# A graph-network layer on one core: bias times std0 as a TensorE product, relu on ScalarE, weights on GpSimd, and another order of issue

## The chip, the cores and the metric

The kernel runs on one core of a Trainium2 chip. The metric is the device time of one execution, in microseconds (us). An iteration below is one turn of the kernel's main loop; a block is ten iterations.

## The reference, cut to what matters

There are 128 graphs of 64 nodes with 128 features, and a 0/1 adjacency matrix for each. An edge (i, j) carries a message, a three-layer network on the two nodes' features; messages of a node's edges are summed, and a second network of the same form updates the node.

```python
def _mlp(x, w0, b0, g0, be0, w1, b1, g1, be1, w2, b2):
    h = _layernorm(jax.nn.relu(x @ w0 + b0), g0, be0)
    h = _layernorm(jax.nn.relu(h @ w1 + b1), g1, be1)
    return h @ w2 + b2
messages = _mlp(concat(f_i, f_j), *msg) * coupling_matrix[..., None]
agg = jnp.sum(messages, axis=2)
updated = x + _mlp(concat(x, agg), *upd)
```

## The kernel before, in words

Only real edges are computed. Two graphs make a pair `p` (64 pairs) with up to 640 edges for each of its graphs; a chunk `n` (160 of them) is 512 edges; five chunks hold two pairs and share one layer-norm step `q`; a block `b` (16) is eight graphs, that is ten chunks. One iteration of the main loop (L721 to L751) issues one chunk's work of every stage, each stage at its own distance: `marks` (which node an edge belongs to, a product on TensorE into the bank `mk`), `compare` (VectorE, makes the 0/1 matrix `s`), `layer0` (two float32r products of 512 columns into `hps`, relu on ScalarE into `h`), `stats0` (four transposes into `hT`, four `bn_stats` on VectorE), `layer1` (four float32 products into `z`, then on VectorE one custom operation that adds `sdb` and takes the relu into `y`, then four `bn_stats`). Here std0 does not divide h: layer 1 is computed on the unnormalized h, and its bias is multiplied by std0 instead. `shift1` makes that product `sdb` on GpSimd, chunk by chunk.

After a step's five chunks, `node_marks` (TensorE) and `weights` (ten ScalarE operations a pair, scaled by 1/std1) give the weights with which `reduce` (20 TensorE instructions a pair) sums y over a node's edges. Per block come the preparation (`load_adj`, `load_x`, `rank`, `count`, `place`, `steps`, `turn`, `rows`) and the update network (`sums_out` to `finish`). `make_tp` (GpSimd) makes a pair's row pointers `tp`.

The order is written out by hand. Each engine executes its instructions in the order of issue. Work beside the chunk stages is put into a plan, `at(n, place, ...)`, and run at iteration `n` in the places `a` (first in the iteration), `m`, `r`, `x`, `x1`, `x2` and `e` (last). `L1`, the distance of layer 1 behind the first chunk stage, is 8. Each of `mk`, `hps`, `hT`, `z`, `ys` and `mu` has one PSUM bank, `ma` has two. Before the loop a prologue prepares block 0; thirteen steps that derive weights (`derive_weights`) run one after another at iterations 1 to 5, and after the loop the overflow flag is computed.

Of the kernel before, what the change touches and what calls it, by code (L numbers as in the profile page):

```python
# [18 lines left out]
EPS = 1e-5  # L19
# [4 lines left out]
def tile_gnn(  # L24
# [82 lines left out]
    nc.vector.memset(eps2_c, EPS * EPS)  # L107
    mean_m = const.tile([P, P], F32, name="mean_m")
    nc.vector.memset(mean_m, 1.0 / C)

# [24 lines left out]
    nc.gpsimd.iota(cmpt[N:P, :], pattern=[[0, 4], [1, CAP]], base=1, channel_multiplier=0,  # L135
                   allow_small_or_imprecise_dtypes=True)
    nc.vector.memset(cmpt[0:N, :], 1.0)
    first = const.tile([P, PB, N], F32, name="first")
    nc.vector.memset(first, 1.0)
    nc.vector.memset(first[:, :, 0:1], 0.0)  # L140

    w0a = mat(mw0[0:C, :], "w0a")
    w0b = mat(mw0[C:2 * C, :], "w0b")
    b0r = row(mb0, "b0r")
    b0c = col(mb0, "b0c")
    w1 = mat(mw1, "w1")
    g0c = col(mg0, "g0c")
    be0c = col(mbe0, "be0c")
    b1r = row(mb1, "b1r")
    w2 = mat(mw2, "w2")  # L150
    g1c = col(mg1, "g1c")
    be1c = col(mbe1, "be1c")
    b2r = row(mb2, "b2r")
    u0a = mat(uw0[0:C, :], "u0a")
    u0b = mat(uw0[C:2 * C, :], "u0b")
    u1 = mat(uw1, "u1")
    u2 = mat(uw2, "u2")
    ub = [row(v, f"ub{i}r") for i, v in enumerate((ub0, ub1, ub2))]
    ug = [col(v, f"ug{i}c") for i, v in enumerate((ug0, ug1))]
    ube = [col(v, f"ube{i}c") for i, v in enumerate((ube0, ube1))]  # L160
# [5 lines left out]
    def derive_weights(bank):  # L166


        def centred(w, g, name):

            wg = const.tile([P, C], F32, name=name + "_g")
            nc.vector.tensor_scalar(wg, w, g, None, op0=ALU.mult)
            ps = bank()
            nc.tensor.matmul(ps[:, :C], lhsT=mean_m, rhs=wg, start=True, stop=True)
            wc = const.tile([P, C], F32, name=name)
            nc.vector.tensor_tensor(wc, wg, ps[:, :C], op=ALU.subtract)
            return wc

        def shift(w, be, bias, name):

            beb = const.tile([P, P], F32, name=name + "_b")
            nc.vector.tensor_copy(beb, be.to_broadcast([P, P]))
            ps = bank()
            nc.tensor.matmul(ps[:, :C], lhsT=beb, rhs=w, start=True, stop=False)
            nc.tensor.matmul(ps[:, :C], lhsT=ones_row, rhs=bias, start=False, stop=True)
            t = const.tile([P, C], F32, name=name)
            nc.vector.tensor_copy(t, ps[:, :C])
            return t

        def spread(bias, name):  # L190
            ps = bank()
            nc.tensor.matmul(ps[:, :C], lhsT=ones_row, rhs=bias, start=True, stop=True)
            t = const.tile([P, C], F32, name=name)
            nc.vector.tensor_copy(t, ps[:, :C])
            return t

        def turned(w, name):
            ps = bank()
            nc.tensor.transpose(ps[:, :C], w, ident)
            t = const.tile([P, C], F32, name=name)  # L200
            nc.vector.tensor_copy(t, ps[:, :C])
            return t

        def times(wT, name):
            ps = bank()
            nc.tensor.matmul(ps[:, :C], lhsT=wT, rhs=u0b, start=True, stop=True)
            t = const.tile([P, C], F32, name=name)
            nc.vector.tensor_copy(t, ps[:, :C])
            return t

        W["w1c"] = centred(w1, g0c, "w1c")
        yield
        W["b1b"] = shift(w1, be0c, b1r, "b1b")
        yield

        w2c = centred(w2, g1c, "w2c")
        yield
        w2cT = turned(w2c, "w2cT")
        yield
        W["w2u"] = times(w2cT, "w2u")  # L220
        yield
        c2b = shift(w2, be1c, b2r, "c2b")
        yield
# [12 lines left out]
        W["cu2b"] = shift(u2, ube[1], ub[2], "cu2b")
# [55 lines left out]
    def edge_path(es):  # L292
# [3 lines left out]
        tpp = es.enter_context(tc.tile_pool(name="tpp", bufs=9))  # L296
        sp = es.enter_context(tc.tile_pool(name="sp", bufs=3))
        hp = es.enter_context(tc.tile_pool(name="hp", bufs=10))
        yp = es.enter_context(tc.tile_pool(name="yp", bufs=12))
        sbp = es.enter_context(tc.tile_pool(name="sbp", bufs=3))  # L300
        wp = es.enter_context(tc.tile_pool(name="wp", bufs=3))
        updp = es.enter_context(tc.tile_pool(name="upd", bufs=1))
        stp = es.enter_context(tc.tile_pool(name="stp", bufs=4))
# [27 lines left out]
        TP, S, H, ST0, V0, SD, SDB, Y, ST1, Q, WT, YS, MK = ({} for _ in range(13))  # L331


        def load_adj(b):
            an = blkp.tile([P, PB, N], F32, name="an", bufs=2)
            nc.sync.dma_start(an, adjp[:, b * PB:(b + 1) * PB, :])
            blocks[b]["an"] = an

        def load_x(b):
            xn = blkp.tile([P, PB, C], F32, name="xn", bufs=5)  # L340
# [155 lines left out]

        def root_of(q):
            SD[q] = root0(stp, V0[q], QT, "m20")

        def shift1(n):  # L500

            q, c = divmod(n, QC)
            SDB[n] = sbp.tile([P, CH, C], F32, name="sdb")
            nc.gpsimd.tensor_tensor(  # L504
                SDB[n], bc(W["b1b"], CH),
                SD[q][:, CH * c:CH * c + CH].unsqueeze(2).to_broadcast([P, CH, C]), op=ALU.mult)

        def layer1(n):
            q, c = divmod(n, QC)
            ps = ps_z.tile([P, CH, C], F32, name="z")  # L510
            h = H.pop(n)
            for t in range(CH):
                nc.tensor.matmul(ps[:, t, :], lhsT=h[:, t * P:(t + 1) * P], rhs=W["w1c"],  # L513
                                 start=True, stop=True)
            Y[n] = yp.tile([P, CH, C], F32, name="y")
            add_relu(Y[n], ps, SDB.pop(n))
            if c == 0:
                ST1[q] = stp.tile([P, QT, 6], F32, name="st1", bufs=2)
            for t in range(CH):
                nc.vector.bn_stats(ST1[q][:, CH * c + t, :], Y[n][:, t, :])  # L520

# [7 lines left out]
        def node_marks(p):  # L529

            WT[p] = []
            for t in range(TG):
                if t % 4 == 0:
                    ps = abank()
                WT[p].append(ps[:, t % 4 * P:(t % 4 + 1) * P])
                nc.tensor.matmul(WT[p][t], lhsT=TP[p][:, t * P:(t + 1) * P],  # L536
                                 rhs=pick.rearrange("p g m -> p (g m)"), start=True, stop=True)
            del TP[p]

        def weights(p):  # L540
# [98 lines left out]
        L1 = QC + 3  # L639
        for b in range(NB):  # L640
            o = b * CPB
            if b > 1:
                at(o - 17, "a", load_adj, b)
                at(o - 13, "a", load_x, b)
            if b > 0:
                at(o - 9, "m", rank, b)
                at(o - 9, "x", count, b)
                at(o - 8, "a", count_out, b)
                at(o - 8, "e", place, b)
# [282 lines left out]
```

## Time and profile before

| | us |
|---|---|
| three runs, median (lowest, highest) | 832.88 (831.65, 836.93) |
| the profiled execution, its own time | 837.1 |
| its span, first to last instruction | 835.4 |
| TensorE busy in the span | 658.4 (79%) |
| VectorE busy | 585.8 (70%) |
| GpSimd busy | 546.6 (65%) |
| ScalarE busy | 341.0 (41%) |

The mean granted TensorE clock is 0.924 of full speed. Matmuls are pipelined and the trace models their ends, so the duration of one is mostly its latency; what a stage costs TensorE in a dense stretch is read from one start to the next. "Idle before" names what an engine waited for.

### The profile page before, as it was taken

Reading aid. Unit: us, or ns where it says so; the run is one execution under the profiler, and the core shown is the slowest. Engines: PE = TensorE matmul, PEld = TensorE weight load, DVE = VectorE, ACT = ScalarE, POOL = GpSimd, SP = SyncE. Lnnn points to the kernel's source line nnn. Section 1 sums busy time; section 2 is a strip of 40 time slices with the busy share of each in tenths; the row PEclk is TensorE's granted clock in tenths of the full one; section 3 lists DMA queues with packets and bytes.
Section 4 is the critical chain, followed back from the end, with each engine's and each line's share of the span. In section 5 each row is a group of like instructions: output and inputs, shape, how many; then the busy total and the mean of one; then the engine's idle time right before and its main releaser. Section 6 shows DMA issues by size and latency. Waiting matters only on the chain.

```text
span 835.4 us, 15966 instructions
## 1 busy us (share of the span) xinstructions
PE 658.4 (79%) x5667; PEld 572.7 (69%) x5667; DVE 585.8 (70%) x1975; ACT 341.0 (41%) x1074; POOL 546.6 (65%) x1003
## 2 busy tenths in 40 slices
PE   4796878887887888788788877878778778878864
PEld 2575767776776787677677766767667666768753
DVE  3468766868677787877678676867768787777722
ACT  2133442444344344434534444444434443443431
POOL 5347555677766676776766667776666777665532
PEclk9999988899899999989999989999999999998966
DMA  3000000010101001010100001010000000000000
GB/s 82 20 1 19 2 1 7 1 33 1 33 2 27 7 2 33 1 33 2 31 2 22 12 2 33 1 33 1 26 8 1 27 2 14 1 13 2 14 10 19
DMA packets 27887, 12.08 MB, mean 14 GB/s; under 512 B 10390, under 2 KB 27804, under 8 KB 27804
## 3 DMA queue, kind: packets, MB, share of 16 engines
q1 hardware_dynamic: 26496, 11.01, 4.9%
q8 instruction: 46, 0.75, 0.4%
q14 instruction: 37, 0.30, 0.1%
q10 hardware_dynamic: 1308, 0.01, 0.1%
HBM read 6.82 MB, written 4.19 MB: 13 GB/s over the span
## 4 chain that ended last, share of the span: by engine, by line
PE 48%; POOL 17%; DVE 16%; ACT 14%; issue 3%; DMA 1%; ACTq 0%; DVEq 0%; POOLq 0%
PE z L513 13%; ACT w L547 7%; PE hps L482 6%; PE hT L491 6%; PE ys L560 6%; PE mk L467 4%; PE mu L589 4%; ACT h L485 4%; PE ma L412 4%; DVE y L245 3%; DVE st L520 3%; DVE st L495 2%; POOL tp L451 2%; DVE s L474 2%; PE mu L426 2%
## 5 line engine op out<-in xcount | busy, mean ns | idle before, releaser
L485 ACT ACTIVATE h<-hps,b0c 128x512 f32<-128x512 f32 x160 | 109.7, 686 | 287.2 <-PE hps L482 287.1
L504 POOL TENSOR_TENSOR sdb<-b1b,m_sd 128x512 f32<-128x512 f32 x160 | 164.6, 1038 | 84.7 <-ACT m_sd L262 84.7
L513 PE MATMUL z<-w1c,h 128*128 128x128 f32 x1280 | 186.2, 292 | 9.6 <-DVE y L245 8.4
L513 PEld LDWEIGHTS z<-w1c,h 128*128 128x128 f32 x1280 | 170.3, 207 | 17.0 <-DVE y L245 16.4
L474 DVE TENSOR_TENSOR s<-mk,cmpt 128x512 fp32r<-128x512 f32 x160 | 109.2, 682 | 80.8 <-PE mk L467 80.5
L495 DVE BATCH_NORM_STATS2 st<-hT 128x6 f32<-128x128 f32 x640 | 141.4, 285 | 4.3 <-PE hT L491 4.3
L520 DVE BATCH_NORM_STATS2 st<-y 128x6 f32<-128x128 f32 x640 | 139.6, 281 | 5.5
L245 DVE CUSTOM_DVE_ANT_0 y<-z,sdb 128x512 f32<-128x512 f32 x160 | 107.4, 671 | 50.3 <-POOL sdb L504 36.1
L547 ACT ACTIVATE w<-ma,m_q 128x64 f32<-128x64 f32 x640 | 137.3, 344 | 2.2 <-PE ma L536 1.8
L451 POOL TENSOR_SCALAR tp<-slot,cumall 128x640 f16<-128x640 f16 x64 | 120.5, 1883 | 0.0
L491 PE MATMUL hT<-ident,h 128*128 128x128 f32 x640 | 111.5, 303 | 7.4 <-ACT h L485 7.4
L491 PEld LDWEIGHTS hT<-ident,h 128*128 128x128 f32 x640 | 86.2, 157 | 30.6 <-ACT h L485 13.9
L252 POOL TENSOR_TENSOR m_d<-st 128x20 f32<-128x20 f32 x64 | 15.9, 249 | 129.8 <-DVE st L520 74.7
L482 PE MATMUL hps<-s,abl 128*128 128x512 f32 (+3 forms) x256 | 96.2, 386 | 0.0
L560 PE MATMUL ys<-y,w 128*64 128x128 f32 x1280 | 87.1, 284 | 0.0
L482 PE MATMUL hps<-s,abh 128*128 128x512 f32 (+3 forms) x256 | 81.0, 335 | 0.0
L560 PEld LDWEIGHTS ys<-y,w 128*64 128x64 f32 x1280 | 71.3, 141 | 9.5 <-issue 4.6
L467 PE MATMUL mk<-tp,qs 128*128 128x512 f16 (+3 forms) x256 | 68.8, 333 | 6.1 <-POOL tp L451 6.1
L536 PE MATMUL ma<-pick,tp 128*128 128x128 f16 x320 | 32.2, 225 | 40.1 <-ACT uhT L418 40.1
L467 PEld LDWEIGHTS <-qs 128*128 128x128 f16 x256 | 21.7, 110 | 52.2 <-issue 49.6
L482 PEld LDWEIGHTS hps<-s,abl 128*128 128x128 f32 x256 | 52.5, 205 | 0.0
L482 PEld LDWEIGHTS hps<-s,abh 128*128 128x128 f32 x256 | 52.1, 204 | 0.0
(166 smaller groups left out, 960.4 us busy)
## 6 DMA issues: line engine op xcount, KB each, us to landing
xn<-in_x_dram SPq DMA_DIRECT2D x16, 256.0 KB, 3.2
out_dram<-uo SPq DMA_DIRECT2D x16, 256.0 KB, 2.4
an<-in_adj_dram SPq DMA_DIRECT2D x16, 128.0 KB, 2.2
w<-in_L_gnn_msg_w_dram SPq DMA_DIRECT2D x2, 64.0 KB, 2.3
u<-in_L_gnn_upd_w_dram SPq DMA_DIRECT2D x2, 64.0 KB, 2.2
w0a<-in_L_gnn_msg_w_dram SPq DMA_DIRECT2D x1, 64.0 KB, 1.8
w0b<-in_L_gnn_msg_w_dram SPq DMA_DIRECT2D x1, 64.0 KB, 2.3
u0a<-in_L_gnn_upd_w_dram SPq DMA_DIRECT2D x1, 64.0 KB, 2.2
```

The lines of the kernel that those rows point to most:

```text
L245: nc.vector._custom_dve(TENSOR_ADD_SAT, out=o, in0=ps, in1=sb, s0=BIG, s1=0.0)
L451: nc.gpsimd.tensor_scalar(tp, slot, cumall[:, p:p + 1], None, op0=ALU.is_lt)
L474: nc.vector.tensor_tensor(S[n], MK.pop(n), cmpt[:, o:o + CH * P], op=ALU.is_equal)
L482: nc.tensor.matmul(ps[:, c:c + w], lhsT=ab[:, g % 4, :], rhs=s[:, c:c + w], start=(k == 0), stop=(k == 1))
L485: nc.scalar.activation(H[n], ps, AF.Relu, bias=b0c)
L491: nc.tensor.transpose(ps[:, t, :], H[n][:, t * P:(t + 1) * P], ident)
L495: nc.vector.bn_stats(ST0[q][:, CH * c + t, :], ps[:, t, :])
L504: nc.gpsimd.tensor_tensor(SDB[n], bc(W["b1b"], CH), SD[q][:, CH * c:CH * c + CH].unsqueeze(2).to_broadcast([P, CH, C]), op=ALU.mult)
L513: nc.tensor.matmul(ps[:, t, :], lhsT=h[:, t * P:(t + 1) * P], rhs=W["w1c"], start=True, stop=True)
L520: nc.vector.bn_stats(ST1[q][:, CH * c + t, :], Y[n][:, t, :])
L547: nc.scalar.activation(w[:, t, g, :], WT[p][t][:, g * N:(g + 1) * N], AF.Copy, scale=Q[q][:, k:k + 1])
L560: nc.tensor.matmul(YS[b][g * N:(g + 1) * N, k, :], lhsT=w[:, t, g, :], rhs=y, start=(t == 0), stop=(t == TG - 1))
```

## The change

- Std0 of a step (80 rows: its 20 tiles, high and low parts, twice) is transposed by TensorE (`root_of`, `turn_root`, `root_out`), and a first product of `layer1` with a table `b1t` (made once, `bias_table`) puts bias times std0 into the bank `z`; the four products add to it. ScalarE takes the relu. `shift1` and the VectorE operation are gone.
- `weights`: ScalarE copies the node marks out (`node_marks_out`, 384 and 256 columns), GpSimd multiplies (two instructions a pair).
- `make_tp` moves from GpSimd to VectorE.
- `L1` is 10; in an iteration the order is `a`, `m`, layer 1, layer 0, stats0, marks and compare (two chunks ahead), stats1, then the rest. Planned steps that hand over to another engine have an iteration between them; the last step is at iteration 193 (183 before). `reduce` of both pairs of a step runs in one iteration.
- The derivation's steps run one an iteration, with their scaling on GpSimd; the flag's steps are planned before the last chunks.
- The first blocks' loads go first, and the small loads move from ScalarE's queue to SP's. Several pools have more buffers.

```diff
-    def col(ap, name, eng=nc.scalar):
+    def col(ap, name, eng=nc.sync):
...
+    load_first(0)
     w0a = mat(mw0[0:C, :], "w0a")
...
+    nc.scalar.activation(eps2_c, eps_c, AF.Sqrt)
+    nc.scalar.activation(eps2_c, eps_c, AF.Square)
...
-            nc.gpsimd.tensor_scalar(tp, slot, cumall[:, p:p + 1], None, op0=ALU.is_lt)
+            nc.vector.tensor_scalar(tp, slot, cumall[:, p:p + 1], None, op0=ALU.is_lt)
...
         def root_of(q):
-            SD[q] = root0(stp, V0[q], QT, "m20")
-
-        def shift1(n):
-
-            q, c = divmod(n, QC)
-            SDB[n] = sbp.tile([P, CH, C], F32, name="sdb")
-            nc.gpsimd.tensor_tensor(
-                SDB[n], bc(W["b1b"], CH),
-                SD[q][:, CH * c:CH * c + CH].unsqueeze(2).to_broadcast([P, CH, C]), op=ALU.mult)
+            sd = root0(stp, V0[q], QT, "m20")
+            SH[q] = lp.tile([P, 4, QT], F32R, name="sh", bufs=2)
+            sdb = sd.unsqueeze(1).to_broadcast([P, 2, QT])
+            nc.scalar.copy(SH[q][:, 0:2, :], sdb)
+            nc.gpsimd.tensor_tensor(SH[q][:, 2:4, :], sdb, SH[q][:, 0:2, :].bitcast(F32),
+                                    op=ALU.subtract)
+
+        def turn_root(q):
+            SD[q] = abank()
+            nc.tensor.transpose(SD[q][0:4 * QT, 0:P],
+                                SH.pop(q).rearrange("p j t -> p (j t)").bitcast(F32), ident)
+
+        def root_out(q):
+            t = lp.tile([4 * QT, P], F32R, name="sdT")
+            nc.scalar.copy(t, SD[q][0:4 * QT, 0:P])
+            SD[q] = t
...
+            nc.tensor.matmul(ps, lhsT=SD[q], rhs=W["b1t"][:, CH * c:CH * c + CH, :], start=True,
+                             stop=False, skip_group_check=True)
             for t in range(CH):
                 nc.tensor.matmul(ps[:, t, :], lhsT=h[:, t * P:(t + 1) * P], rhs=W["w1c"],
-                                 start=True, stop=True)
+                                 start=False, stop=True, skip_group_check=True)
             Y[n] = yp.tile([P, CH, C], F32, name="y")
-            add_relu(Y[n], ps, SDB.pop(n))
+            nc.scalar.activation(Y[n], ps, AF.Relu)
+
+        def stats1(n):
...
+        def node_marks_out(p):
+            o = wp.tile([P, TG, 2, N], F16, name="oh")
+            for ps, t, n in zip(OH[p], (0, 3), (3, TG - 3)):
+                nc.scalar.copy(o[:, t:t + n].rearrange("p t g m -> p (t g m)"), ps[:, 0:n * P])
+            OH[p] = o
+
         def weights(p):
...
-            for t in range(TG):
-                for g in range(2):
-                    k = (2 * h + g) * TG + t
-                    nc.scalar.activation(w[:, t, g, :], WT[p][t][:, g * N:(g + 1) * N], AF.Copy,
-                                         scale=Q[q][:, k:k + 1])
+            for g in range(2):
+                k = (2 * h + g) * TG
+                nc.gpsimd.tensor_tensor(
+                    w[:, :, g, :], OH[p][:, :, g, :],
+                    Q[q][:, k:k + TG].unsqueeze(2).to_broadcast([P, TG, N]), op=ALU.mult)
...
-        L1 = QC + 3
+        L1 = 2 * QC
...
+            w = p // 2 * QC + L1 + QC + p % 2
+            at(w + 1, "x", node_marks, p)
+            at(w + 2, "a", node_marks_out, p)
+            at(w + 3, "e1", weights, p)
+            at(p // 2 * QC + L1 + 2 * QC, "x1", reduce, p)
         for q in range(NQ):
...
+            n = q * QC + QC
+            at(n, "e1", var0_of, q)
+            at(n + 2, "a", root_of, q)
+            at(n + 3, "x", turn_root, q)
+            at(n + 4, "a", root_out, q)
+            at(n + L1, "e1", var1_step, q)
+            at(n + L1 + 2, "a", root1_of, q)
+            at(n + L1 + 2, "m", inverse_of, q)
...
         for n in range(last + 1):
             run(n, "a")
+            run(n, "m")
+            if 0 <= n - L1 < NCHK:
+                layer1(n - L1)
             if n < NCHK:
...
+                layer0(n)
+            if 0 <= n - 1 < NCHK:
+                stats0(n - 1)
+            if n + 2 < NCHK:
+                marks(n + 2)
+                compare(n + 2)
+            if 0 <= n - L1 < NCHK:
+                stats1(n - L1)
+            for k in ("x", "x1", "x2", "e1", "e"):
                 run(n, k)
```

## Rows read from the trace of the kernel before

**Rows 1.** Page: busy time (share) and instructions of each engine.

```profile
PE 658.4 (79%) x5667; PEld 572.7 (69%) x5667; DVE 585.8 (70%) x1975; ACT 341.0 (41%) x1074; POOL 546.6 (65%) x1003
```

**Rows 2.** Timeline of ScalarE: relu of chunks 0, 10, 60, 70, 159.

```profile
20.42 0.69 ACT L485 ACTIVATE h<-hps,b0c 128x512 f32<-128x512 f32 x1 [0.80 <-PE hps L482]
...
65.07 0.69 ACT L485 ACTIVATE h<-hps,b0c 128x512 f32<-128x512 f32 x1 [1.53 <-PE hps L482]
...
301.84 0.69 ACT L485 ACTIVATE h<-hps,b0c 128x512 f32<-128x512 f32 x1 [0.49 <-PE hps L482]
...
349.56 0.69 ACT L485 ACTIVATE h<-hps,b0c 128x512 f32<-128x512 f32 x1 [0.49 <-PE hps L482]
...
774.50 0.69 ACT L485 ACTIVATE h<-hps,b0c 128x512 f32<-128x512 f32 x1 [0.93 <-PE hps L482]
```

**Rows 3.** Stretches of 4 us: busy PE, PEld, DVE, ACT, POOL; clock, DMA.

```profile
316.00:320.00 4.00, 1.59 (x9) 1.36 (x7) 1.24 (x6) 2.92 (x12) 3.87 (x6) 0.83 0.34 90
320.00:324.00 4.00, 4.00 (x28) 3.02 (x28) 3.06 (x11) 1.66 (x4) 4.00 (x4) 0.75 0.00 0
...
332.00:336.00 4.00, 4.00 (x53) 3.54 (x52) 3.93 (x14) 0.69 (x1) 1.26 (x6) 1.00 0.00 0
```

**Rows 4.** Waits: who waited for whom, us in total, times, longest.

```profile
PEld ma L412 <- ACT w L547: 91.1, 44, 2.9
POOL sdb L504 <- ACT m_sd L262: 84.7, 32, 3.3
```

**Rows 5.** Timeline of TensorE in a dense stretch (start, duration).

```profile
341.27 0.42 PE L482 MATMUL hps<-s,abl 128*128 128x384 f32 x1
...
341.87 1.10 PE L589 MATMUL mu<-u1c,uhT 128*128 128x128 f32 x8
342.81 0.38 PE L467 MATMUL mk<-tp,qs 128*128 128x512 f16 x1
343.03 0.60 PE L491 MATMUL hT<-ident,h 128*128 128x128 f32 x4
343.46 1.06 PE L513 MATMUL z<-w1c,h 128*128 128x128 f32 x8
344.27 0.48 PE L482 MATMUL hps<-s,abl 128*128 128x512 f32 x1
344.59 0.40 PE L482 MATMUL hps<-s,abh 128*128 128x512 f32 x1
344.83 0.46 PE L536 MATMUL ma<-pick,tp 128*128 128x128 f16 x5
345.21 1.31 PE L560 MATMUL ys<-y,w 128*64 128x128 f32 x20
346.36 0.27 PE L426 MATMUL mu<-w0a,xnT 128*64 128x128 f32 x1
...
347.33 0.39 PE L467 MATMUL mk<-tp,qs 128*128 128x128 f16 x2
```

**Rows 6.** Page: groups of instructions: busy us, mean ns of one, idle before.

```profile
L485 ACT ACTIVATE h<-hps,b0c 128x512 f32<-128x512 f32 x160 | 109.7, 686 | 287.2 <-PE hps L482 287.1
L504 POOL TENSOR_TENSOR sdb<-b1b,m_sd 128x512 f32<-128x512 f32 x160 | 164.6, 1038 | 84.7 <-ACT m_sd L262 84.7
...
L474 DVE TENSOR_TENSOR s<-mk,cmpt 128x512 fp32r<-128x512 f32 x160 | 109.2, 682 | 80.8 <-PE mk L467 80.5
L495 DVE BATCH_NORM_STATS2 st<-hT 128x6 f32<-128x128 f32 x640 | 141.4, 285 | 4.3 <-PE hT L491 4.3
...
L245 DVE CUSTOM_DVE_ANT_0 y<-z,sdb 128x512 f32<-128x512 f32 x160 | 107.4, 671 | 50.3 <-POOL sdb L504 36.1
L547 ACT ACTIVATE w<-ma,m_q 128x64 f32<-128x64 f32 x640 | 137.3, 344 | 2.2 <-PE ma L536 1.8
L451 POOL TENSOR_SCALAR tp<-slot,cumall 128x640 f16<-128x640 f16 x64 | 120.5, 1883 | 0.0
```

**Rows 7.** Timeline of the head: the first operation of the edge path.

```profile
7.56 0.69 DVE L348 TENSOR_TENSOR_SCAN rk<-first,an 128x256 f32<-128x256 f32 x1 [3.12 <-DMA an<-in_adj_dram]
```

More of the change, by code (lines that the diff above doesn't have):

```diff
@@ L134, in tile_gnn @@
     cmpt = const.tile([P, 4 * CAP], F16, name="cmpt")
[L135 to L160, printed above, removed]
+    ones_row = const.tile([1, P], F32, name="ones_row")
+    nc.vector.memset(ones_row, 1.0)
+    mean_m = const.tile([P, P], F32, name="mean_m")
+    nc.vector.memset(mean_m, 1.0 / C)
     cumall = const.tile([P, NP], F32, name="cumall")
@@ L164, in tile_gnn, with derivation, product, empty @@
     W = {}
-    def derive_weights(bank):
+    def derivation(bank):
         def centred(w, g, name):
             wg = const.tile([P, C], F32, name=name + "_g")
[L172 to L177, printed above, removed]
+            nc.gpsimd.tensor_scalar(wg, w, g, None, op0=ALU.mult)
+            def product():
+                ps = bank()
+                nc.tensor.matmul(ps[:, :C], lhsT=mean_m, rhs=wg, start=True, stop=True)
+                return ps
+            def empty(ps):
+                W[name] = const.tile([P, C], F32, name=name)
+                nc.vector.tensor_tensor(W[name], wg, ps[:, :C], op=ALU.subtract)
+            return product, empty
+        def plain(name, fn):
+            def product():
+                ps = bank()
+                fn(ps[:, :C])
+                return ps
+            def empty(ps):
+                W[name] = const.tile([P, C], F32, name=name)
+                nc.vector.tensor_copy(W[name], ps[:, :C])
+            return product, empty
@@ L197, in turned @@
-        def turned(w, name):
[L198 to L211, printed above, removed]
@@ L330, in edge_path @@
         blocks = {b: {} for b in range(NB)}
-        TP, S, H, ST0, V0, SD, SDB, Y, ST1, Q, WT, YS, MK = ({} for _ in range(13))
+        TP, S, H, ST0, V0, SD, SH, Y, ST1, Q, OH, WT, YS, MK = ({} for _ in range(14))
         def load_adj(b):
-            an = blkp.tile([P, PB, N], F32, name="an", bufs=2)
+            if b < 2:
+                blocks[b]["an"] = an0[:, b]
+                return
+            an = blkp.tile([P, PB, N], F32, name="an", bufs=3)
             nc.sync.dma_start(an, adjp[:, b * PB:(b + 1) * PB, :])
@@ L681, in edge_path @@
-            at(u + 10, "m", finish, b)
+            u = o + L1 + 3 * QC
+            at(u + 1, "a", sums_out, b)
+            at(u + 3, "e", bias0, b)
+            at(u + 4, "x", turn, b, "ysum")
+            at(u + 5, "a", turn_out, b, "ysum")
+            at(u + 6, "x", lambda b: layer(b, ("xnT", u0a), ("ysumT", W["w2u"])), b)
+            at(u + 7, "m", layer_out, b, "uh", "m0")
+            at(u + 7, "e", upd_m0, b)
+            at(u + 9, "a", upd_root0, b)
+            at(u + 9, "e", upd_shift, b)
@@ L696, in edge_path @@
-        for n in range(13):
-            at(1 + n // 3, "e", next, derivation, None)
+            if n >= 4:
+                at(n - 4, "m", make_tp, p)
+            w = p // 2 * QC + L1 + QC + p % 2
[3 more added lines that the diff above has]
+            at(p // 2 * QC + L1 + 2 * QC, "x1", reduce, p)
+        for q in range(NQ):
+            n = q * QC + QC
[6 more added lines that the diff above has]
+            at(n + L1 + 2, "m", inverse_of, q)
@@ L704, in edge_path @@
         rank(0)
+        turn(0, "xn")
+        turn_out(0, "xn", 5)
         count(0)
         count_out(0)
+        nc.vector.memset(cmpt[0:N, :], 1.0)
+        rows(0, 0)
+        rows_hi(0, 0)
         place(0)
@@ L716, in edge_path, with keep, flag_in, flag_turn @@
         steps_out(0)
-        odd_weights(0)
-        marks(0)
+        nc.gpsimd.iota(cmpt[N:P, :], pattern=[[0, 4], [1, CAP]], base=1, channel_multiplier=0,
+                       allow_small_or_imprecise_dtypes=True)
+        marks(0)
+        compare(0)
+        marks(1)
+        compare(1)
+        odd_weights(0)
+        for n, (product, empty) in zip([n for n in range(1, 20) if n % QC], derivation(ubank)):
+            def keep(n=n, product=product):
+                W["ps", n] = product()
+            at(n, "x", keep)
+            at(n + 1, "m", lambda n=n, empty=empty: empty(W.pop(("ps", n))))
+        at(3, "e", bias_table)
+        fl = const.tile([P, 2], F32, name="fl")
+        f2 = const.tile([2, 1], F32, name="f2")
+        flag = const.tile([1, 1], I32, name="flag")
+        FL = {}
+        def flag_in():
+            nc.vector.tensor_reduce(fl[:, 0:1], cumall, axis=AX.X, op=ALU.max)
+            nc.vector.tensor_scalar(fl[:, 0:1], fl[:, 0:1], CAP + 0.5, None, op0=ALU.is_gt)
+            nc.vector.tensor_reduce(fl[:, 1:2], nball, axis=AX.X, op=ALU.max)
+            nc.vector.tensor_scalar(fl[:, 1:2], fl[:, 1:2], 0.0, None, op0=ALU.is_gt)
+        def flag_turn():
+            FL["a"] = ubank()
+            nc.tensor.transpose(FL["a"][0:2, 0:P], fl, ident)
+        def flag_max():
+            nc.vector.tensor_reduce(f2, FL["a"][0:2, 0:P], axis=AX.X, op=ALU.max)
+        def flag_sum():
+            FL["b"] = ubank()
+            nc.tensor.matmul(FL["b"][0:1, 0:1], lhsT=f2, rhs=mean_m[0:2, 0:1], start=True,
+                             stop=True)
+        def flag_out():
+            nc.vector.tensor_scalar(flag, FL["b"][0:1, 0:1], float(C), None, op0=ALU.mult)
+        at(NCHK - 8, "m", flag_in)
+        at(NCHK - 7, "x", flag_turn)
+        at(NCHK - 6, "m", flag_max)
+        at(NCHK - 2, "x", flag_sum)
+        at(NCHK - 1, "m", flag_out)
         last = max(n for n, _ in plan)
```

266 lines of the change are left out of this document (125 added, 141 removed).

## Prediction

> **What bounds the kernel now.** The first view is the page's busy time: TensorE leads with 658.4 of 835.4 us, VectorE has 585.8, GpSimd 546.6, and no engine is full [rows 1]. The second is ScalarE's timeline of the relu of layer 0, one a chunk, which serves as a clock: chunk 0 at 20.42, chunk 10 at 65.07, chunk 159 at 774.50, and between chunks 60 and 70 it takes 47.72 us a block [rows 2]. So the span is 65 us of head and first block, 709 for 149 chunks at 4.77 each, and 60.9 of tail.
>
> The third view cuts the steady part into stretches of 4 us. In 316 to 320 TensorE was busy 1.59 us; in the stretch behind that it was busy throughout, at a granted clock of 0.75, so part of it at 1.2 GHz; in 332 to 336 it was busy throughout at 1.00, 2.4 GHz [rows 3]. Pauses are paid twice: as idle time, and as a lower clock after them. The waits name them: TensorE's transposes into `ma` wait 91.1 us for ScalarE's weights, which hold both banks of `ma`, and GpSimd waits 84.7 us for std0, at 3.3 us at most, 32 times: a serial chain from the last stats0 over square sum and root to `sdb` [rows 4].
>
> The fourth view is a dense stretch of TensorE at full clock, which gives each stage's price from one start to the next [rows 5]: marks 0.22, four transposes 0.43, layer 1 0.81, layer 0 0.56 in one piece and 0.60 in two (I take 0.60), node marks 0.38, reduce 1.15 a pair, half a block's rows 0.97, eight instructions of the update 0.94. Per block: ten chunks at 2.06, 20.6; four reduces 4.6; rows 1.9; update 32 instructions 3.8; node marks 1.5; 16 more transposes 1.7; small products, an estimate, 0.6. That is 34.7 of 47.7 us. **TensorE's own work bounds nothing yet; 13 us a block are pauses and slow clock**, made by hand-overs inside an iteration.
>
> **The change, part by part.**
>
> *Bias product.* One float32r product of 512 columns a chunk. The two such products of layer 0 show 0.32 (next start after the first) and 0.24 (after the second) [rows 5]; I take 0.27. Above, it could cost what four float32 products of 128 columns do, 0.81; below, nothing, were it to lie wholly in a pause. Ten a block: 2.7 (0 to 8.1). A transpose of std0 per step adds 0.1, so TensorE comes to 34.7 + 2.7 + 0.2 = 37.6 us a block. It waits for `sdT`, and behind it in TensorE's queue stand layer 0, the transposes and the marks; the chain (square sum in iteration 5q+5, root 5q+7, transpose 5q+8, copy 5q+9, use 5q+10) has an iteration of about 4 us for steps of at most some 2, so I cost the wait at nothing; if it were late, the whole iteration would stand.
>
> *VectorE.* `y` goes, 107.4 us; `tp` comes, 64 times [rows 6]. No such VectorE row exists: above, 640 columns at the rate of the compare (682 ns for 512) are 0.85, below I leave 0. The compare is the nearest row, so 0.85: 54 us. (585.8 - 107.4 + 54.4)/16 = 33.3 us a block, under TensorE's 37.6.
>
> *ScalarE.* Off: weights 137.3. On: 160 relus of 512 columns from PSUM at 686 ns, 109.7; node marks, 640 columns a pair at that rate 0.86, 55; roots' copies, an estimate of 0.5 a step, 16 [rows 6]. 341.0 becomes 385, 24 a block: hidden, if `a` work doesn't hold the relu of `z` back.
>
> *GpSimd.* Off: `sdb` 164.6 and `tp` 120.5. On: 128 multiplications of 320 columns, 0.65 at the rate of `sdb` (1038 ns for 512), 0.94 at that of `tp` (1883 for 640) [rows 6]; the input is f16 as in `tp`, so 0.9: 115; subtractions, about 8. 546.6 becomes 385, 24 a block, hidden. `weights` come one and two iterations ahead of `reduce`; behind them on GpSimd wait `bias0` and `upd_shift`, needed four and three iterations later.
>
> *Order.* What remains is whether TensorE runs dense. With one bank per stage, its transposes of iteration n+1 wait for VectorE's stats0 of iteration n, and they come 1.08 + 0.60 = 1.7 us into the iteration; marks wait for the compare before. Base work per iteration is TensorE 2.3 and VectorE 2.4 (compare 0.68, twice four statistics at 0.22 apart). Two iterations in ten hold both reduces and the rows, TensorE 5.6, and VectorE idles there. The heaviest for VectorE is the seventh (the update's add and relu with four statistics, as `y` and stats0 show them, 1.55; rank 0.7 [rows 7]; the reciprocal, an estimate, 0.3): 4.9 against 2.7. Up to 1.7 us of lateness is absorbed, so 0.5 is left there, about 0.5 in the next, and I allow as much again elsewhere: 1.8. **Steady: 37.6 + 1.8 = 39.4 us a block** instead of 47.7. With no long pause the clock should stay at the 1.00 of [rows 3]. The DMA waits of the buffers lie 20 to 25 iterations ahead, out of the way.
>
> *Head.* Block 0's adjacency is loaded first; its rank now waits for the DMA until 7.56 [rows 7] and gains about 4 us. Two `tp` of 1.88 leave the chain, but the iota of `cmpt` (64 x 2560) moves behind `place`. Chunk 0 at 15 instead of 20.4 (11 to 21). The derivation, five iterations of serial hand-overs, becomes one step an iteration; thirteen small loads go behind each other on SP's queue, hidden by the work of block 0, needed from iteration 1 on. Without layer 1 an iteration holds TensorE 1.3 to 2.2, VectorE 1.6 to 2.6; 2.7 with hand-overs at a lower clock: 27 for ten, where before took 44.65 (22 to 40). Iterations 10 to 29 lack reduce and update work at first: 30 + 35.
>
> *Tail.* Ten more planned iterations, but empty ones cost only their hand-overs. Iterations 160 to 169 are bound by the one bank `z` (product 1.08, drain, relu 0.69: 2.1) or by TensorE's extras: 25. Then root, weights, reduces and the update's chain of two blocks, about 31, and 2 from the last relu on: 58, against 60.9 (50 to 70).
>
> **Sum.** 15 + 27 + 65 + 13 x 39.4 (512) + 58 = 677 span. The profiled execution was 837.1 with a span of 835.4: 1.7 around it, 678.7. The median of the runs, 832.88, stands 0.5% under that execution; 678.7 scaled by it is **675 us**.
>
> **Rivals.**
>
> *Lock step.* TensorE and VectorE don't overlap across iterations, each iteration takes the longer of both. The excess of VectorE over TensorE, by rows: seventh 2.2, third (the output, an estimate, 0.9, `tp` 0.85) 1.3, second (update, inverse) 0.6, eighth 0.7, sixth 0.4: 5.2, so 37.6 + 5.2 = 42.8, plus hand-overs 43.2; 13 x 43.2 + 165, and 6 more in the ramp: 733 span, 731 by the median. For it: one bank for every stage; before shows TensorE's pauses from just such coupling. Against: marks run two chunks ahead, every step has an iteration to spare.
>
> *`tp` against GpSimd.* Before, `tp` and all of GpSimd's work share no VectorE operation of that kind, so no row prices a collision. Above, each of four `tp` a block waits for one GpSimd operation of 1.04 (as `sdb`): with lock step 43.2 + 4.2 = 47.4, 13 x 47.4 + 171 = 787, 785 by the median. Below, nothing. The Trainium skill ("SBUF — State Buffer", Who interferes with whom) says that VectorE's `tensor_scalar` in a 2-port mode and GpSimd lock each other out of a shared port pair for a whole instruction. By that rule, which speaks against this move, the time comes out here; no row of before shows the lock. Lighter GpSimd (24 of 39 us) makes most of it free.
>
> *Slower: GpSimd's weights bind.* Its other work is 16.3 a block plus 0.5; eight multiplications decide above (39.4 - 16.8)/8 = 2.8 us each, and give slower than before from 13b + 165 = 841, b = 52, so 4.4 each. For it: an f16 input broadcast over 64 columns, a form without a row. At 4.9 each, 13 x 56 + 165 = 893, 890 by the median. Against: the dearest GpSimd row per column, `tp`, gives 0.94.
>
> *The pauses stay.* If the relu on ScalarE waits as the `y` on VectorE did, 47.7 stays, with the bias product outweighed by the head: within 1%.
>
> **How the numbers follow.** Dense TensorE, 643 to 700: 0.70. Lock step with or without collisions, 700 to 790: 0.23. The weights or another new wait that binds an engine: 0.05. Pauses that stay: 0.02. The range has TensorE's 37.6 and a quick head below (489 + 22 + 13 + 62 + 56 = 642), the lock step above (735), and leaves the collisions and the slow case out. 1% is about what a measurement of this kernel tells from no change: faster 0.93, within 1% 0.02, slower 0.05.
>
> **What would show it.** Right: blocks 39 to 41 us apart in the relu's timeline; the clock at 0.98 or above in the steady part; TensorE over 90% busy there; GpSimd and VectorE near 385 and 530 in all; weights under 1 us, `tp` under 0.85, the bias product 0.24 to 0.32 to the next start. Lock step would show as TensorE's transposes waiting for stats0; a collision as `tp` long before or after a GpSimd operation; a late `sdT` as layer 1 waiting for ScalarE. Wrong: blocks above 43, or a tail well over 70.

## The result, and the profile after

The changed kernel takes **654.3 us** (median of 4, 650.9 to 655.8) where the kernel before took 832.8 on the same chip: a ratio of 0.784 (0.780 to 0.789). The forecast was 675, in a range of 642 to 735. The profiled execution has a span of 653.6. Beside experiments 5 to 8 the kernel before took 834 to 838 us in ten runs and 822 in one, so the ratios given there have wide intervals.

The page's first part, as in [rows 1]:

```profile
PE 624.3 (96%) x5859; PEld 573.4 (88%) x5859; DVE 496.4 (76%) x1871; ACT 349.3 (53%) x788; POOL 377.5 (58%) x956
```

TensorE went from 79% of a long span to 96% of a short one; VectorE lost 89 us of work and GpSimd 169. ScalarE's relu of layer 0 is the clock again, as in [rows 2], here at chunks 0, 10, 70, 80 and 159:

```profile
16.63 0.69 ACT L489 ACTIVATE h<-hps,b0c 128x512 f32<-128x512 f32 x1 [5.19 <-PE hps L486]
...
45.95 0.68 ACT L489 ACTIVATE h<-hps,b0c 128x512 f32<-128x512 f32 x1
...
256.71 0.68 ACT L489 ACTIVATE h<-hps,b0c 128x512 f32<-128x512 f32 x1
...
293.97 0.68 ACT L489 ACTIVATE h<-hps,b0c 128x512 f32<-128x512 f32 x1
...
587.02 0.68 ACT L489 ACTIVATE h<-hps,b0c 128x512 f32<-128x512 f32 x1
```

A block went from 47.72 to 37.26 us (37.25 between chunks 60 and 70): 10.5 times some 13 blocks is 136 of the 179 gained. Chunk 10 comes 19 us earlier, and the tail behind chunk 159 is 66.6, 6 longer than before. Where [rows 3] had pauses and a granted clock of 0.75 behind them, a stretch of 100 us has none; the two stretches under it are the end of the tail (columns as in [rows 3]):

```profile
300.00:400.00 100.00, 100.00 (x972) 93.60 (x971) 81.80 (x310) 58.62 (x134) 57.82 (x154) 1.00 0.08 21
630.00:640.00 10.00, 6.41 (x28) 5.59 (x26) 2.86 (x10) 1.82 (x5) 6.17 (x14) 0.58 0.01 2
640.00:653.60 13.60, 5.26 (x20) 4.28 (x20) 2.88 (x11) 1.09 (x3) 2.77 (x9) 0.50 0.14 41
```

Who waits for whom (the view of [rows 4]) has turned round. Engines now wait for TensorE, or for each other in slack time; the two waits of [rows 4] are gone:

```profile
POOL sh L510 <- ACT sh L509: 116.9, 31, 6.4
ACT y L534 <- PE z L531: 86.4, 130, 3.5
...
DVE st L499 <- PE hT L495: 55.0, 92, 2.6
```

The new operations, in the view by groups with shapes kept apart (as [rows 6]):

```profile
L534 ACT ACTIVATE y<-z 128x512 f32<-128x512 f32 x160 | 95.7, 598 | 87.4 <-PE z L531 86.4 <-DVE s L478 1.0
L605 POOL TENSOR_TENSOR w<-oh,m_q 128x320 f32<-128x320 f16 x128 | 89.9, 725 | 3.2 <-PE ma L589 1.0 <-DVE m_q L279 1.0 <-PE hT L495 0.4
...
L455 DVE TENSOR_SCALAR tp<-slot,cumall 128x640 f16<-128x640 f16 x64 | 31.2, 489 | 0.4 <-ACT cumall L366 0.4
```

And a bias product with its neighbours in TensorE's timeline (start, duration; as [rows 5]):

```profile
264.99 0.48 PE L528 MATMUL z<-b1t,sdT 80*128 80x512 f32 x1
265.30 1.05 PE L531 MATMUL z<-w1c,h 128*128 128x128 f32 x8
266.11 0.36 PE L486 MATMUL hps<-s,abl 128*128 128x256 f32 x1
```

0.31 from the bias product to the next start, 0.81 for layer 1 behind it. Over chunks 30 to 149 the first is 0.33 in the mean.

### The profile page after: what moved, and what is told of

Read it like the earlier page. It is cut to its first block, busy times and chain, and to the rows that moved or that the text cites. A ratio compares the mean times of both kernels' runs of the same rounds, so it can differ in the third digit from the quotient of the medians.

```text
span 653.6 us, 15818 instructions
## 1 busy us (share of the span) xinstructions
PE 624.3 (96%) x5859; PEld 573.4 (88%) x5859; DVE 496.4 (76%) x1871; ACT 349.3 (53%) x788; POOL 377.5 (58%) x956
## 5 line engine op out<-in xcount | busy, mean ns | idle before, releaser
L531 PE MATMUL z<-w1c,h 128*128 128x128 f32 x1280 | 168.9, 275 | 0.0
L541 DVE BATCH_NORM_STATS2 st<-y 128x6 f32<-128x128 f32 x640 | 137.8, 277 | 10.8 <-ACT y L534 10.8
L534 ACT ACTIVATE y<-z 128x512 f32<-128x512 f32 x160 | 95.7, 598 | 87.4 <-PE z L531 86.4
L495 PE MATMUL hT<-ident,h 128*128 128x128 f32 x640 | 98.1, 276 | 1.7 <-DVE st L499 1.7
L605 POOL TENSOR_TENSOR w<-oh,m_q 128x320 f32<-128x320 f16 x128 | 89.9, 725 | 3.2 <-PE ma L589 1.0
L495 PEld LDWEIGHTS hT<-ident,h 128*128 128x128 f32 x640 | 76.9, 142 | 12.3 <-DVE st L499 2.4
L596 ACT CAST oh<-ma 128x384 f16<-128x384 f32 (+1 forms) x128 | 48.2, 429 | 61.9 <-PE ma L589 61.1
L528 PE MATMUL z<-b1t,sdT 80*128 80x512 f32 x160 | 78.9, 493 | 1.9 <-ACT y L534 1.9
L620 PE MATMUL ys<-y,w 128*64 128x128 f32 x1280 | 78.2, 275 | 1.0 <-POOL w L605 1.0
L510 POOL TENSOR_TENSOR sh<-m_sd,sh 128x40 fp32r<-128x40 f32 x32 | 8.7, 271 | 116.9 <-ACT sh L509 116.9
L446 DVE TENSOR_TENSOR abl<-mu,abh 128x512 fp32r<-128x512 f32 x32 | 22.1, 691 | 53.2 <-ACT abh L439 53.2
```

Of the source, the lines that this page charges most:

```text
L495: nc.tensor.transpose(ps[:, t, :], H[n][:, t * P:(t + 1) * P], ident)
L528: nc.tensor.matmul(ps, lhsT=SD[q], rhs=W["b1t"][:, CH * c:CH * c + CH, :], start=True, stop=False, skip_group_check=True)
L534: nc.scalar.activation(Y[n], ps, AF.Relu)
L605: nc.gpsimd.tensor_tensor(w[:, :, g, :], OH[p][:, :, g, :], Q[q][:, k:k + TG].unsqueeze(2).to_broadcast([P, TG, N]), op=ALU.mult)
L620: nc.tensor.matmul(YS[b][g * N:(g + 1) * N, k, :], lhsT=w[:, t, g, :], rhs=y, start=(t == 0), stop=(t == TG - 1))
```

## The experiments

Theory: the hand-written order made TensorE dense, and the moves between engines gave it only room. Rivals: the moves themselves did it; or the bias product, or `tp` on VectorE against GpSimd, holds the kernel where it is. Blocks are read between chunks 60 and 70.

**1. Without the bias product.**

```
-            nc.tensor.matmul(ps, lhsT=SD[q], rhs=W["b1t"][...], start=True, stop=False, ...)
+            # the four products of layer 1 start the bank themselves
```

> The changed kernel without the bias product in layer 1 (the term bias times std0 is left out; its chain stays). Theory: the steady part is bound by TensorE alone, 37.26 us a block, busy throughout; a chunk loses 0.31 us from the product's start to the next one's, 160 of them 50 us, so a span near 604, up to 615 if the next product starts later. Rival, lock step or hand-overs set the pace: the span stays above 640, since VectorE, ScalarE and GpSimd keep their work.

Measured 624.7 (ratio 0.748, 0.744 to 0.752), a span of 625.7 and a block of 35.62: 1.64 less, 0.16 a chunk, half of what the next start showed. So neither expectation held: the span lies between the two. Where the rest went is read from one start to the next in TensorE's timelines of both kernels, over chunks 30 to 149. The bias products took 3.30 a block. Without them layer 1 takes 8.54 where it took 8.10, the transposes and the wait ahead of them 0.67 more, and smaller products 0.5 more: 1.66 net. One layer 1 without a product ahead of it, at the slower end:

```profile
266.81 1.16 PE L529 MATMUL z<-w1c,h 128*128 128x128 f32 x8
267.72 0.31 PE L486 MATMUL hps<-s,abl 128*128 128x128 f32 x1
```

It takes 0.91; in the steady part these lie between 0.81 and 1.09, 0.86 in the mean, and with the bias product always at 0.81 or 0.82. That a weight load which lay under the long product now stands by itself would explain this; no run shows it alone. And a wait that the changed kernel hardly has (2.4 us there):

```profile
PEld hT L495 <- DVE st L499: 11.2, 27, 1.9
```

TensorE's transposes wait for stats0, 0.7 a block. That is the lateness by VectorE that the forecast walked through; with the bias product in, TensorE is slow enough to hide it.

**2. The old division in the new order**: `sdb` on GpSimd and `y` as VectorE's add and relu; no bias product.

```
-            nc.tensor.matmul(ps, lhsT=SD[q], rhs=W["b1t"][...], ...)   # and turn_root, root_out
-            nc.scalar.activation(Y[n], ps, AF.Relu)
+            add_relu(Y[n], ps, SDB.pop(n))     # SDB[n] = b1b * std0 on GpSimd, an iteration ahead
```

> The changed kernel with bias and relu as before (GpSimd makes sdb for each chunk, VectorE adds and takes the relu; no bias product, no transposed roots), in the new order. Theory, the order made most of the gain: TensorE 34 us a block, VectorE 30.2 + 6.7 = 36.9, GpSimd 22.5 + 10.4 = 33, so VectorE with its coupling to TensorE sets 37 to 40, total 645 to 690. Rival, the new division of the work made the gain: 760 or more.

Measured 675.3 (0.811, 0.808 to 0.813), a block of 38.68. The stretch of 100 us and the first wait:

```profile
300.00:400.00 100.00, 93.22 (x920) 85.81 (x920) 93.24 (x325) 41.63 (x91) 84.60 (x174) 1.00 0.08 21
```

```profile
PEld z L522 <- DVE y L243: 65.1, 70, 1.9
```

VectorE is as full as TensorE, which waits for it. The bias product and its relu are worth 21 us, by taking this work off VectorE, though the product alone costs 30.

**3. `tp` back on GpSimd.**

```
-            nc.vector.tensor_scalar(tp, slot, ...)          # place "m"
+            (nc.vector if p < 2 else nc.gpsimd).tensor_scalar(tp, slot, ...)   # place "e"
```

> The changed kernel with tp made on GpSimd again (all but the first two pairs), new order. Theory: GpSimd comes to 22.5 + 7.5 = 30 us a block, under TensorE's 37.26, VectorE falls to 28; the time stays within 1% of 654. Rival, the move itself was worth something because GpSimd's queue delays weights or square sums: above 670.

Measured 654.8 (0.786, 0.784 to 0.789), blocks of 37.24: this move is worth nothing here.

**4. All the new parts in the old order** (old sequence in the iteration, old distances in the plan; the new steps put beside the ones they replace; the loads, the derivation, the buffers and `L1` = 8 are those of the kernel before).

> The kernel before with the new division of the work (bias product, relu on ScalarE, node marks out and weights on GpSimd, tp on VectorE) in the old order and at the old distances. Theory, the order made most of the gain: pauses stay where a hand-over falls into one iteration (root to transpose, weights to reduce, marks to compare), 740 to 820. Rival, the division made it: 660 to 720.

Measured 807.9 (0.971, 0.967 to 0.975). A block is 45.90. **The new division by itself, in the old order, is worth 3%.**

**5 and 6. A mixed division.** `sdb` for two chunks of ten (and for four, with `tp` on GpSimd) as before, without a bias product there.

```
+        OWN = (0, 5)          # run 6: (0, 4, 5, 9)
...
+            if n % (2 * QC) in OWN:
+                ...           # layer 1 alone, then add_relu(Y[n], ps, SDB.pop(n)) on VectorE
```

> The changed kernel with two chunks of ten (the first of each five, in TensorE's long iterations, where VectorE idles) on the old way: sdb from GpSimd, add and relu on VectorE, no bias product. Theory, TensorE sets the pace: e1 gave 0.16 us net a chunk and 0.31 gross, so 0.3 to 0.6 us a block, 645 to 650. Rival, VectorE's lateness eats it: 654 or more.

> Four chunks of ten on the old way (first and last of each five), and tp on GpSimd, which takes 2 us a block off VectorE. Theory: 0.7 to 1.2 us a block less on TensorE, 636 to 645, with GpSimd at 34 us a block. Rival, GpSimd's queue becomes late for weights or sdb: 654 or more.

Measured 648.1 (644.9 to 648.4) and 656.3 (653.7 to 656.9). Two of ten gain about 1%: a block is 36.80, 0.45 less. With four and `tp`, GpSimd is 90% busy in the steady stretch and TensorE 99% instead of 100%. The second was a miss for the theory, and its rival held: VectorE's add waits 56.2 us for `sdb` from GpSimd.

**7. The weights back on ScalarE**, from PSUM, one iteration earlier to feed the same reduce.

```
-                nc.gpsimd.tensor_tensor(w[:, :, g, :], OH[p][:, :, g, :], Q[q][...]..., op=ALU.mult)
+                    nc.scalar.activation(w[:, t, g, :], ps[...], AF.Copy, scale=Q[q][:, k:k + 1])
```

> The changed kernel with the weights made on ScalarE from PSUM as before (ten operations a pair, 2.15 us), root and reciprocal of std1 one iteration earlier. Theory: ScalarE has 27 us a block, but in the iterations with weights its work ahead of the relu of z grows from 1.7 to 3.0 us, so z's one bank holds TensorE back by 0.5 to 1 us four times a block: 670 to 700. Rival, with the new order the place of the weights is worth nothing: 654.

Measured 673.7 (0.814, 0.800 to 0.827), a block of 38.52 with TensorE at 98 to 99%. Layer 1's weight loads now wait 21.9 us for ScalarE's relu, 39 times, since it holds the one bank `z` (the changed kernel: 2.8), as the theory had it.

**8 and 9. The order, half by half.** Run 8 keeps the plan's new distances and puts back the old sequence of places in an iteration; run 9 keeps the new sequence and puts back the old distances, as here:

```
-            u = o + L1 + 3 * QC                      # updates: 18 iterations a block
+            u = o + CPB + L1 + QC                    # 10
-            at(n + 2, "a", root_of, q)
-            at(n + 3, "x", turn_root, q)
-            at(n + 4, "a", root_out, q)
+            at(n + 4, "a", root_of, q)
+            at(n + 4, "x", turn_root, q)
+            at(n + 5, "a", root_out, q)              # used in iteration n + 5
```

> The changed kernel with the sequence of before inside an iteration (compare first, stats0 ahead of layer 1, layer 0 behind it, marks last) and the new distances of the plan. Theory, both the distances and the sequence matter, the distances most: the transposes of stats0 come first in TensorE's iteration and wait for the relu of the layer 0 that was last in it, 0.3 to 0.6 us in the short iterations: 665 to 700. Rival, the sequence alone made the gain: above 760.

> The changed kernel with the new sequence of the places inside an iteration, and every distance of the plan (hand-overs, blocks' steps, updates, quarters) as it was before the change. With old sequence and old distances the new parts gave 808, with old sequence and new distances 691, with both new 654. Theory that the distances are the larger half and the sequence adds to them: 808 less the 37 that the sequence was worth, 760 to 790. Rival that the sequence alone would have done most of it (each engine's stretch ends with work that waits for nothing): below 710. If the two need each other: 795 or more.

Measured 691.4 (0.835, 0.819 to 0.850) and **814.7** (0.976, 0.971 to 0.980). With run 4 this fills a square; in brackets stands the steady part alone, the time from the relu of chunk 30 to that of chunk 159:

| | old distances | new distances |
|---|---|---|
| old sequence | 807.9 (590.9) | 691.4 (505.1) |
| new sequence | 814.7 (612.9) | 654.3 (478.5) |

The relu of chunks 30 and 159 in runs 4, 8 and 9, and of chunk 30 in the changed kernel:

```profile
148.90 0.68 ACT L485 ACTIVATE h<-hps,b0c 128x512 f32<-128x512 f32 x1
...
739.81 0.68 ACT L485 ACTIVATE h<-hps,b0c 128x512 f32<-128x512 f32 x1
```

```profile
117.27 0.68 ACT L489 ACTIVATE h<-hps,b0c 128x512 f32<-128x512 f32 x1
...
622.36 0.68 ACT L489 ACTIVATE h<-hps,b0c 128x512 f32<-128x512 f32 x1
```

```profile
132.47 0.69 ACT L489 ACTIVATE h<-hps,b0c 128x512 f32<-128x512 f32 x1 [0.26 <-PE hps L486]
...
745.42 0.68 ACT L489 ACTIVATE h<-hps,b0c 128x512 f32<-128x512 f32 x1
```

```profile
108.56 0.68 ACT L489 ACTIVATE h<-hps,b0c 128x512 f32<-128x512 f32 x1
```

The right column and the lower row are clean: their two kernels differ in the sequence alone, or in the distances alone. With the new sequence the distances are worth 160 us, 134 of them in the steady part; with the new distances the sequence is worth 37, 27 of them in the steady part. Run 4 differs from its neighbours in more: it keeps the old head (chunk 10 comes at 63.14, in run 9 at 44.97), the old buffers and `L1` = 8. So the 117 us between runs 4 and 8 hold more than the distances; 86 lie in the steady part. Between runs 4 and 9 the better head hides that the steady part got 22 us longer. The theory had 760 to 790; the third case that it named came, 795 or more: the two need each other. In run 8 the sequence costs mostly this wait, which the changed kernel's list doesn't have:

```profile
PEld hT L495 <- ACT h L489: 29.3, 53, 0.8
```

The waits of run 4 and of run 9 show what the new sequence does with the old distances:

```profile
PEld z L520 <- ACT sdT L513: 53.6, 32, 3.2
```

```profile
DVE st L499 <- PE hT L495: 155.5, 100, 4.3
ACT y L534 <- PE z L531: 153.4, 106, 3.5
POOL m_d L250 <- DVE st L499: 129.7, 31, 6.0
...
PEld z L528 <- ACT sdT L520: 102.5, 32, 4.4
```

The new sequence puts layer 1 first in the iteration. With the old distances `sdT` is copied in that same iteration, so TensorE stands for it 3.2 us a step instead of 1.7, 49 us more in all, and nothing behind it in its queue can go ahead. That this wait is what turns the sequence's gain into a loss is read from the waits and wasn't tried by itself.

**10. The tail: the last two updates pulled in.** 21 steps in 10 and 7 iterations in place of 18, for blocks 14 and 15.

```
+            D = (1, 3, 4, ... 17, 18) if b < NB - 2 else (1, 1, 4, ... 9, 10) if b < NB - 1 else (1, 1, 1, ... 6, 7)
-            at(u + 4, "x", turn, b, "ysum")       # and the other steps
+            at(u + D[2], "x", turn, b, "ysum")
```

> The changed kernel, with the update steps of the last two blocks of 512 nodes pulled together (21 steps in 10 and in 7 iterations in place of 18), so that the first of the two is done before the second begins. Theory that the tail's 40 us after the last layer 1 (31 were predicted) come from two updates one after the other in order: the tail after the last relu of layer 0 falls from 66.6 to 57 to 62, and the time to 645 to 650. Rival that the tail is the latency of one chain at the low clock, whatever stands beside it: 652 to 656.

Measured 655.1 (0.785, 0.782 to 0.788), a miss; the tail is 66.5, as long as before. First the changed kernel (ScalarE: last relu of layer 1, the last block's sums, block 14's root, the copy behind it), then run 10 (GpSimd, then ScalarE):

```profile
613.46 0.60 ACT L534 ACTIVATE y<-z 128x512 f32<-128x512 f32 x1 [1.29 <-PE z L531]
...
626.87 0.59 ACT L629 COPY ysum<-ys 128x512 f32<-128x512 f32 x1 [2.93 <-PE ys L620]
631.16 0.30 ACT L274 ACTIVATE um_sq<-um_v,eps_c 128x4 f32<-128x4 f32 x1 [3.71 <-POOL um_v L268]
631.37 0.56 ACT L422 COPY uyT<-ma 128x512 f32<-128x512 f32 x1
631.83 0.59 ACT L422 COPY ysumT<-ma 128x512 f32<-128x512 f32 x1
```

```profile
626.07 0.20 POOL L250 TENSOR_TENSOR um_d<-uy_st 128x4 f32<-128x4 f32 x1 [2.48 <-DVE uy_st L659]
...
627.40 1.40 POOL L605 TENSOR_TENSOR w<-oh,m_q 128x320 f32<-128x320 f16 x2
...
633.30 0.59 ACT L629 COPY ysum<-ys 128x512 f32<-128x512 f32 x1 [5.05 <-PE ys L620]
```

In the changed kernel the last sums come 13.4 us after the last layer 1, and then the last block's chain stands behind block 14's root: 26.7 to the end. In run 10 the last weights stand on GpSimd behind block 14's square sum, which waits 2.48 for VectorE, and the last reduces on TensorE behind block 14's third layer; the sums come 6.4 later, and the chain, now undisturbed and at a clock of 0.93 from 630 to 640 (0.58 in the changed kernel), needs 20.1. The time fell in the rival's range, 652 to 656. But the chain got shorter, so the stall was there and came back in another place; run 12 tests that.

**11. Best of the runs so far**: run 5, run 10's tail, and GpSimd's iota for `cmpt` issued in the set-up.

> Three edits together: sdb of two chunks of ten (n mod 5 = 0) back on GpSimd as a product with an add on VectorE and no bias product there (648 alone), the last two updates pulled together, and GpSimd's iota for the compare's constants issued in the set-up, where the first compare waited 3.97 us for it. If the three add up: 648 less 5 to 8 less 2 to 3, 637 to 641. If the tail is one chain's latency and the head is set by something behind the iota: 646 to 650.

Measured 644.9 (644.5 to 646.0; 0.773, 0.770 to 0.775). This lies between the two expectations. Chunk 0 comes at 14.22, 2.4 earlier: the iota counted. The tail is 65.7, so pulling the updates in gained as little as in run 10.

**12. The end written by hand.** After the last layer 1 the steps stand one by one; the rest is run 11 without the pulled-in distances.

```
+        node_marks(r + 2)        # last quarter's marks, root and inverse ahead of the updates
+        uy_out(x); var1_step(q); finish(x)
+        node_marks_out(r + 2); root1_of(q); inverse_of(q)
+        ...                      # weights, reduces; block 14's second layer in the gaps of 15's first
```

> As the run with three edits (644.9), but what is left after the last layer 1 is in an order written step by step instead of pulled-in distances: the last quarter's marks and its root go ahead of the updates, so that the last block's sums are ready at about 10 us after the last layer 1 and not at 13 (changed kernel) or 20 (updates pulled in), and block 14's second layer runs in the gaps of block 15's first. Theory that the tail is the way to the last sums plus one chain of about 20 us: last relu of layer 0 to the end 57 to 60 in place of 66.6, the time 635 to 640. Rival that the low clock and the waits for two blocks' shared buffers set it: 643 to 647.

Measured **634.0** (633.5 to 634.8), 0.761 (0.758 to 0.763) of the kernel before and 3% under the changed kernel. ScalarE's copy of the last sums, and two stretches of the end:

```profile
602.16 0.60 ACT L553 ACTIVATE y<-z 128x512 f32<-128x512 f32 x1 [1.29 <-PE z L551]
...
614.87 0.59 ACT L648 COPY ysum<-ys 128x512 f32<-128x512 f32 x1 [1.05 <-PE ys L639]
```

```profile
610.00:620.00 10.00, 8.27 (x92) 7.04 (x88) 2.67 (x9) 2.84 (x6) 9.01 (x20) 1.00 0.00 0
620.00:632.00 12.00, 4.51 (x32) 3.58 (x30) 4.53 (x18) 1.66 (x4) 4.72 (x15) 0.76 0.16 49
```

The sums come 12.7 after the last layer 1 (10 were expected), and from there to the end it is 17.1 (about 20 were expected) instead of 26.7. The tail is 55.8, a little under the 57 to 60 expected and 10.8 under the changed kernel's 66.6. So the sums came hardly earlier, and it is the chain behind them that got shorter. Part of that is the clock. In the changed kernel TensorE waits 2.35 us for `ysumT`; the granted clock is at 1.00 (2.4 GHz) until 631.5, falls in this wait, and is 0.50 (1.2 GHz) behind it. A stretch inside that wait, its end, the last block's second layer there, and the same layer in run 12:

```profile
631.50:632.00 0.50, 0.00 (x0) 0.00 (x0) 0.17 (x1) 0.50 (x2) 0.50 (x1) 0.64 0.00 0
```

```profile
632.47 0.80 PE L649 MATMUL mu<-w2u,ysumT 128*128 128x128 f32 x2 [2.35 <-ACT ysumT L422]
...
640.37 2.08 PE L649 MATMUL mu<-u1c,uhT 128*128 128x128 f32 x8 [0.73 <-ACT uhT L422]
```

```profile
622.19 1.13 PE L668 MATMUL mu<-u1c,uhT 128*128 128x128 f32 x8 [0.93 <-ACT um_sd L262]
```

Over the three layers the lower clock costs some 2.6 us (an estimate from their starts and the starts behind them in both timelines); the other 7 of the 9.6 are mostly waits in the queues, such as the copy of `ysumT` behind block 14's root. No run changes the clock alone.

## Why the prediction was right

*What bounds.* Right: pauses and slow clock went, and TensorE's own work is what remains. Its sum from [rows 5], 37.6 a block, is met by 37.26. Read from start to start over chunks 30 to 149, the bias products take 3.30 a block (2.7 taken) and node marks 1.01 (1.5), two errors that cancel; small products take 0.4 (0.6), and every other term lies within 0.2 of its forecast.

*Order.* Right in kind, mis-sized: the 1.8 us of stalls a block aren't there (100.00 of 100 us busy). The term was VectorE's seventh iteration, put at 4.9 us against TensorE's 2.7: 1.7 absorbed, 0.5 left there, 0.5 in the next, and as much again elsewhere. The trace has 4.44 from one stats0 to the next there, against TensorE's 2.59 from one layer 1 to the next, and the 1.85 between them is absorbed:

```profile
282.54 0.89 DVE L499 BATCH_NORM_STATS2 st<-hT 128x6 f32<-128x128 f32 x4 [0.72 <-PE hT L495]
...
286.98 0.82 DVE L499 BATCH_NORM_STATS2 st<-hT 128x6 f32<-128x128 f32 x4
```

```profile
283.75 0.48 PE L528 MATMUL z<-b1t,sdT 80*128 80x512 f32 x1
...
286.34 0.47 PE L528 MATMUL z<-b1t,sdT 80*128 80x512 f32 x1
```

`tp` took 0.49 where 0.85 was forecast, which makes 23 of the 34 by which VectorE's total of 496 stayed under 530. Experiment 1 shows that the lateness is real as soon as TensorE has 1.64 us a block less to do. 0.34 and 1.8 over 13 blocks are 28 of the 33.5 by which chunks 30 to 159 came out under the 512 of the sum; 3.7 more are a chunk that I counted in the 512 and in the tail. So one sign named beforehand was missed, on the good side: blocks at 39 to 41.

*Bias product.* 0.27 taken, 0.33 to the next start in the mean, but 0.16 net: without it layer 1 takes longer and the wait for stats0 comes up (experiment 1). *Relu* 598 ns, not 686; *weights* 0.725, not 0.9, within their bounds of 0.65 and 0.94: both hidden.

*Head and ramp.* Rank starts at 3.11, as forecast 4 earlier, and chunk 0 at 16.63 (15):

```profile
3.11 0.69 DVE L352 TENSOR_TENSOR_SCAN rk<-first,an 128x256 f32<-128x256 f32 x1 [1.45 <-DMA an<-in_adj_dram]
...
14.41 0.69 DVE L478 TENSOR_TENSOR s<-mk,cmpt 128x512 fp32r<-128x512 f32 x1 [3.97 <-POOL cmpt L782]
```

The iota that the forecast named without a price held the first compare 3.97; experiment 11 got 2.4 back. Iterations 0 to 9 took 29.3 (27), 10 to 29 took 62.6 (65).

*Tail.* The step that failed: 58 forecast, 66.6 measured. Iterations 160 to 169 took the 25 of the sum. The "31" behind them was 40: it named the chain of two blocks, but wasn't worked out from rows, and left out that the two updates stand in each other's way on four queues in order. Experiment 12 shows the term without that: 29.8 behind the last layer 1, 55.8 for the tail.

*The sum.* The span came out 23.4 under the 677: steady part 33.5 and ramp 2.4 less, chunk 0 1.6, the first ten iterations 2.3 and the tail 8.6 more. So the mechanism was right, but that the time came within 3% is in part luck, as errors of both signs met.

*Rivals.* The lock step (43.2 a block) is refuted in the changed kernel. `tp` against GpSimd happens, and costs nothing that the end sees: 30 of 64 `tp` took 0.37 to 0.38, the others 0.46 to 0.84, and one in the ramp 1.99. That one, in the timelines of GpSimd and VectorE of the changed kernel:

```profile
30.22 4.47 POOL L570 TENSOR_TENSOR b1t<-b1mix,tile_of 80x2560 fp32r<-80x2560 f32 x1
```

```profile
32.89 1.99 DVE L455 TENSOR_SCALAR tp<-slot,cumall 128x640 f16<-128x640 f16 x1
```

It ends at 34.88, 0.19 after GpSimd's long operation (30.22 + 4.47 = 34.69). With the Trainium skill ("SBUF — State Buffer", Who interferes with whom), which has a VectorE operation in a 2-port mode and GpSimd lock each other out for a whole instruction, the row agrees. The mean excess over 0.38 is 0.11 us, 7 us over all 64 on an engine that isn't full, and experiment 3 finds nothing to gain by avoiding it. That GpSimd's weights bind is refuted by 725 ns. Experiment 4 stands nearest to "the pauses stay": with the new parts in the old order they do, at 3% gain. Not tried by themselves are the two iterations more of `L1`, the larger buffers and the order of the loads.

## What to carry to other kernels

When every engine is under 80% busy, look first at how many iterations lie between a hand-over's producer and its consumer, and set those before the sequence inside an iteration: here the distances gave 160 us with the new sequence, and the sequence gave 37 only on top of them; without them the steady part was 22 longer with it (experiments 4 and 9). Moving work between engines pays after that, up to the point where the bound engine is dense, and then work given back to engines with room (experiment 5) is the next per cent. A kernel's end is its own schedule: price it with the updates in each other's way, and let what the last result waits for go first on every queue.

## What was not expected of the hardware

A float32r product of 512 columns ahead of float32 layers of 128 showed 0.33 us to the next start in the mean and gained 0.16 when taken away. The transposes and products of several kinds that stand in a dense stretch held the granted clock at 1.00 (2.4 GHz) throughout (300 to 400 us). At the end of the changed kernel it fell to 0.50 (1.2 GHz) in a wait of 2.35 us, while in experiment 12 it was still 1.00 from 610 to 620, with TensorE busy 8.27 us of 10. VectorE's `is_lt` on f16, 640 columns, took 0.37 to 0.38 us in 30 of 64 cases, where GpSimd took 1.88 for the same [rows 6].
